# Layer 3's closing dot products as rows in column quarters of the array, two phases exchanged, and a new written order for layers 2 and 3 of a graph network

## The chip, the cores and the metric

The kernel runs on one core of a Trainium2 chip. The metric is the device time of one launch, in microseconds (us). The time before is 651.76 us, the median of three runs (651.25 to 652.19). The core has five engines that work side by side, each with its own instruction queue in program order: PE (TensorE, matrix products; its weight loads are listed as PEld), DVE (VectorE), ACT (ScalarE), POOL (GpSimd) and SP (SyncE, which here issues the DMA transfers).

## The reference, cut to what matters

Four graph layers run over the same 3327 nodes with 64 features and the same weighted adjacency matrix; each adds its result to x. Layer 0 is a gated graph convolution (two rounds), layer 1 a hyperbolic one, layer 2 one in which each row's neighbours are weighted by their rank from the end. The change is in layers 2 and 3. Layer 3, cut down:

```python
def _L3_gnn_ref(x, adj, att_W, att_b):
    x_tan = _logmap0(x, C)
    left = x_tan @ att_W[:D] + att_b
    right = x_tan @ att_W[D:]
    adj_att = jax.nn.sigmoid(left + right.T) * adj
    x_local = _logmap(x[:, None, :], x[None, :, :], C)
    support_t = jnp.einsum('ij,ijd->id', adj_att, x_local)
    return _proj(_expmap(x, support_t, C), C)
# layer 2
rank = jnp.cumsum(mask, axis=1)
w = mask * jnp.where(pos > 0, DECAY ** (k - pos), 0.0)
out = w @ (input @ weight) + bias
```

The logarithm map of a pair (i, j) depends on three inner products: of i with itself, of j with itself and of i with j. So the sum over j becomes a sum S_i of scaled neighbour vectors plus a single number d_i. What ends the layer is worked out per node from d_i and two dot products over the 64 features: h_i·S_i and S_i·S_i.

## The kernel before

**Nodes and groups.** The nodes are padded to 26 blocks of 128. Two blocks at a time are one column block c (0 to 12): the 128 partitions of a transposed tile hold the 64 features of both. Group 0 (`gs_`, the small group) is c = 0 to 5, group 1 (`gf`, the large one) c = 6 to 12.

**Layer 2.** For each of 52 steps n (26 source blocks for each group) there are: `mask` (L1784, DVE: which entries of an adjacency tile are set), `count` (L1815, PE: ranks by triangular products, into one of two PSUM pairs; then ACT or DVE turns ranks into powers of two, L1827 or L1825) and `weigh` (L1837, PE: these weights times the support rows, in two parts). The support itself is made by a chain of small steps, `support` (L1013 to L1063), a Python generator that a helper named `Weave` advances between the steps of a loop; the loop's `flush` holds a `weigh` back until its support is done. Up to step 27 this loop sets the order.

**Layer 3.** The symmetric pairs of column blocks are split into 13 `PHASES`; each phase names its direct columns (target ts from source c) and, derived from them, the turned ones (target c from source ts). For each phase m, half b and chunk there are `distances` (L1354, PE), `gelus` and `square` (ACT, or DVE), `tanh_d` and `tanh_t` (L1395, L1424, ACT), `attention_d` and `attention_t` (L1435, DVE, with the adjacency tile), `factors_d` (L1453, DVE), `turned` (L1469, PE transposes), `factors_t` (L1476, DVE), `gather_d`, `gather_t` and `singles` (all recorded at L1479, PE). The gathers add to S in four PSUM banks: `x0` and `x1` for the large group, `x2_` for blocks 0 to 3 and part of `ps_` for blocks 4 and 5. `singles` add the numbers d to 32-row quarters of `ps_`, four products beside each other in four quarters of the array's columns; those of the last phase's second half go to a bank of their own, `late_`, cleared by L1284.

**The order.** From step 28 of layer 2 on, the order of all these calls is a list written out by hand, `ORDER3`. An entry such as `gather_t.12.0.1` calls that step; `n`, `s`, `b`, `f` advance generators: `nodes3` of the two groups (normalisation, transposes, tables of layer 3; the small group's use POOL, L1145 to L1243), a bound, and `finish_f`. Each engine executes its part of the list in this order, so an instruction that waits holds up all behind it on its engine. The adjacency tiles are loaded by SP in the order in which `mask` and `attention` use them (`uses_of_tiles`), and a slot is filled again once its user is done.

**The end.** `finish_f` copies the large group's S to SBUF, multiplies it by the transposed h (`w1`) and squares it (`w2`), forms the dots with `added` (L1587: each block of w1 or w2 as 128-column weights, a moving operand `halves` of two columns that pick the upper and lower 64 features), and transposes S to node order (`by_nodes`, L1598). These steps stand in the list as `f`. After the list, `finish` does the same for the small group, copies the late single sums (`copied_singles`, L1604), brings them to node order (`picked`, L1609), and runs a chain of some 35 small DVE operations (L1656 to L1693) that ends in two scale factors per node; with these, ACT scales h (L1703), PE adds x (L1701, L1705) and DVE forms the output (L1708 to L1719), which SP stores.

Of the kernel before, what the change touches and what calls it, by code (L numbers as in the profile page):

```python
# [45 lines left out]

SLOTS3, SLOTS2, SLOTS1, SLOTS01 = 4, 7, 16, 19
# [126 lines left out]
for _c in range(0, 6, 2):  # L174
# [4 lines left out]
    Phase((0, r_(0, 4)), (1, r_(1, 4))),  # L179
    Phase((0, r_(4, 6)), (1, r_(4, 6)), (4, r_(4, 6)), (5, r_(5, 6))),  # L180
    Phase((2, r_(2, 6)), (3, r_(3, 6))),
# [21 lines left out]
def uses_of_tiles():  # L203

    last_first = [2 * c + h for c in reversed(range(HB)) for h in range(2)]
    layer2 = [(g, k) for g in (1, 0) for k in last_first]
    rest = []
    for name, *args in ORDER3:
        if name == "mask":
            rest.append(layer2[args[0]])  # L210
        elif name.startswith("attention"):
            rest.append((*args, name == "attention_t"))
    listed = sum(len(key) == 2 for key in rest)
    starts, uses = [], []
    for u in (
        FIRST + SECOND + THIRD + LAYER1,
        layer2[:NB],
        layer2[NB : len(layer2) - listed] + rest,
    ):
        starts.append(len(uses))  # L220
        uses += u
    return uses, starts[1:]
# [5 lines left out]
def order3(text):  # L228
# [14 lines left out]
    count.28.0 mask.30 count.28.1 mask.31 n n weigh.26.0 weigh.26.1 count.29.0 count.29.1 n  # L243
    n weigh.27.0 n weigh.27.1 count.30.0 count.30.1 weigh.28.0 weigh.28.1 weigh.29.0
    count.31.0 count.31.1 weigh.30.0 mask.32 mask.33 n weigh.29.1 count.32.0 mask.34
    count.32.1 weigh.30.1 weigh.31.0 count.33.0 count.33.1 mask.35 weigh.31.1 count.34.0
    count.34.1 weigh.32.0 weigh.32.1 weigh.33.0 weigh.34.0 n count.35.0 count.35.1 mask.36
    weigh.33.1 weigh.34.1 mask.37 count.36.0 weigh.35.0 count.36.1 count.37.0 n n n n n n
    weigh.36.0 weigh.35.1 mask.38 mask.39 count.37.1 mask.40 n n n count.38.0 count.38.1
    weigh.36.1 n weigh.37.0 count.39.0 weigh.37.1 mask.41 count.39.1 weigh.38.0 mask.42  # L250
    count.40.0 count.40.1 n weigh.38.1 count.41.0 weigh.39.0 weigh.39.1 weigh.40.0
    count.41.1 weigh.40.1 mask.43 count.42.0 count.42.1 n n n n weigh.41.0 weigh.41.1 n
    mask.44 mask.45 mask.46 count.43.0 count.43.1 n n n count.44.0 count.44.1 mask.47
    weigh.42.0 weigh.43.0 n n weigh.42.1 count.45.0 n n n mask.48 count.45.1 n weigh.43.1
    weigh.44.0 count.46.0 count.46.1 mask.49 weigh.44.1 count.47.0 n n n tanh_t.0.0.0
    count.47.1.1 weigh.45.0 n weigh.45.1 count.48.0 count.48.1 mask.50 weigh.46.0 mask.51
    weigh.46.1 count.49.0 weigh.47.0 tanh_t.0.0.1 tanh_t.0.1.0 count.49.1.1 weigh.47.1
    count.50.0 weigh.48.0 count.50.1.1 tanh_d.0.0 weigh.49.0 tanh_t.0.1.1 weigh.48.1
    count.51.0 count.51.1.1 weigh.49.1 distances.0.0.0 attention_t.0.0 gelus.0.0.0
    distances.0.0.1 weigh.50.0 weigh.51.0 gelus.0.0.1 attention_d.0.0 square.0.0 weigh.50.1  # L260
    weigh.51.1 wk evict distances.0.1.0 s s s tanh_t.1.0.0 gelus.0.1.0 tanh_d.0.1
    distances.1.0.0 gelus.1.0.0 distances.0.1.1 s clear.2 distances.1.0.1 gelus.0.1.1 s
    clear.1 factors_d.0.0 clear.0 square.0.1 gelus.1.0.1 gather_d.0.0 s s turned.0.0.0
    factors_t.0.0.0 distances.1.1.0 gather_t.0.0.0 turned.0.0.1 attention_t.0.1
    factors_t.0.0.1 gather_t.0.0.1 singles.0.0 s s tanh_d.1.0 turned.0.1.0 gelus.1.1.0
    factors_t.0.1.0 distances.1.1.1 s turned.0.1.1 attention_d.0.1 factors_d.0.1 square.1.0
    factors_t.0.1.1 gelus.1.1.1 distances.2.0.0 s s tanh_t.1.1.0 gather_t.0.1.0 s
    attention_t.1.0 attention_d.1.0 s s gelus.2.0.0 distances.2.0.1 s s square.1.1
    gather_t.0.1.1 turned.1.0.0 factors_t.1.0.0 tanh_d.1.1 attention_t.1.1 s s gather_d.0.1
    gelus.2.0.1 distances.2.1.0 factors_d.1.0 tanh_d.2.0 singles.0.1 gather_t.1.0.0  # L270
    gelus.2.1.0 turned.1.1.0 factors_t.1.1.0 square.2.0 distances.2.1.1 tanh_t.2.0.0
    gelus.2.1.1 s tanh_t.2.0.1 s gather_d.1.0 square.2.1 distances.3.0.0 s gelus.3.0.0
    gather_t.1.1.0 attention_d.1.1 factors_d.1.1 tanh_t.2.1.0 turned.2.0.0 distances.3.0.1
    gelus.3.0.1 tanh_t.2.1.1 singles.1.0 distances.3.1.0 square.3.0 attention_t.2.0
    factors_t.2.0.0 turned.2.0.1 gather_t.2.0.0 gelus.3.1.0 distances.3.1.1 attention_d.2.0
    factors_d.2.0 s s factors_t.2.0.1 turned.2.1.0 tanh_d.2.1 gelus.3.1.1 s gather_d.2.0
    tanh_t.3.0.0 tanh_t.3.0.1 distances.4.0.0 s s singles.2.0 singles.1.1 attention_t.2.1
    attention_d.2.1 factors_d.2.1 gelus.4.0.0 square.3.1 s s s factors_t.2.1.0 turned.2.1.1
    factors_t.2.1.1 distances.4.0.1 attention_t.3.0 turned.3.0.0 factors_t.3.0.0 tanh_d.3.0
    attention_d.3.0 s gather_d.1.1 s s turned.3.0.1 factors_t.3.0.1 gelus.4.0.1 s  # L280
    distances.4.1.0 s gather_t.2.1.0 tanh_t.3.1.0 gather_t.2.0.1 gather_t.3.0.0 tanh_t.3.1.1
    turned.3.1.0 factors_d.3.0 gelus.4.1.0 tanh_d.3.1 attention_t.3.1 attention_d.3.1
    tanh_d.4.0 s distances.4.1.1 gelus.4.1.1 factors_t.3.1.0 tanh_t.4.0.0 gather_d.2.1
    tanh_t.4.0.1 gather_d.3.0 gather_t.3.0.1 factors_d.3.1 singles.2.1 b turned.3.1.1
    attention_t.4.0 factors_t.3.1.1 distances.5.0.0 b gather_d.3.1 square.4.1
    attention_d.4.0 gelus.5.0.0 gather_t.3.1.0 square.4.0 tanh_t.4.1.0 gather_t.2.1.1
    distances.5.0.1 gelus.5.0.1 turned.4.0.0 tanh_t.4.1.1 z factors_t.4.0.0 distances.5.1.0
    factors_d.4.0 turned.4.0.1 singles.3.1 factors_t.4.0.1 tanh_d.4.1 gelus.5.1.0 square.5.0
    attention_t.4.1 singles.3.0 tanh_t.5.0.0 tanh_t.5.0.1 turned.4.1.0 attention_d.4.1
    factors_t.4.1.0 factors_d.4.1 distances.5.1.1 gather_t.4.0.1 gather_t.4.0.0 gather_d.4.0  # L290
    gather_t.3.1.1 turned.4.1.1 factors_t.4.1.1 gelus.5.1.1 attention_t.5.0 distances.6.0.0
    singles.4.0 tanh_d.5.0 attention_d.5.0 square.5.1 turned.5.0.0 gelus.6.0.0
    distances.6.0.1 tanh_t.5.1.0 tanh_t.5.1.1 gelus.6.0.1 factors_t.5.0.0 attention_t.5.1
    gather_t.4.1.1 tanh_d.5.1 gather_d.4.1 turned.5.0.1 distances.6.1.0 gather_t.4.1.0
    tanh_t.6.0.0 factors_t.5.0.1 gather_t.5.0.1 factors_d.5.0 gelus.6.1.0 turned.5.1.0
    square.6.0 distances.6.1.1 gelus.6.1.1 factors_t.5.1.0 singles.4.1 turned.5.1.1
    distances.7.0.0 attention_d.5.1 gather_t.5.0.0 tanh_t.6.0.1 factors_t.5.1.1
    gather_t.5.1.1 attention_t.6.0 square.6.1 turned.6.0.0 factors_t.6.0.0 gelus.7.0.0
    distances.7.0.1 gather_t.5.1.0 tanh_t.6.1.0 turned.6.0.1 gelus.7.0.1 tanh_d.6.0
    distances.7.1.0 factors_d.5.1 gelus.7.1.0 tanh_t.6.1.1 factors_t.6.0.1 attention_d.6.0  # L300
    singles.5.0 tanh_t.7.0.0 turned.6.1.0 attention_t.6.1 factors_t.6.1.0 tanh_d.6.1
    attention_d.6.1 distances.7.1.1 gather_d.5.0 gather_t.6.0.0 gather_t.6.0.1 gelus.7.1.1
    gather_t.6.1.0 gather_d.5.1 turned.6.1.1 tanh_t.7.0.1 distances.8.0.0 square.7.1
    square.7.0 factors_d.6.0 singles.6.0 factors_t.6.1.1 gelus.8.0.0 factors_d.6.1
    tanh_d.7.0 singles.5.1 attention_t.7.0 tanh_t.7.1.0 attention_d.7.0 singles.6.1
    turned.7.0.0 tanh_d.7.1 distances.8.0.1 gelus.8.0.1 gather_d.6.0 tanh_t.7.1.1
    factors_t.7.0.0 gather_t.7.0.0 tanh_t.8.0.0 tanh_t.8.1.0 factors_d.7.0 turned.7.0.1
    factors_t.7.0.1 attention_t.7.1 attention_d.7.1 distances.8.1.0 gelus.8.1.0
    gather_t.6.1.1 gather_d.7.0 turned.7.1.0 factors_t.7.1.0 tanh_t.8.0.1 distances.8.1.1
    singles.7.0 turned.7.1.1 tanh_d.8.0 gelus.8.1.1 distances.9.0.0 factors_d.7.1  # L310
# [107 lines left out]
def gnn_kernel(ctx: ExitStack, tc: tile.TileContext, t, out):  # L418
# [663 lines left out]

    ROWS = (HB + 1) // 2

    def by_halves(a):  # L1090
        return a.rearrange("p (c a) -> p a c", a=2)

    def gelu_table():

# [525 lines left out]
    def finish_f():  # L1620
# [9 lines left out]
        for lo in range(0, g.n, 2):  # L1630
            added(g, ws_, lo, min(lo + 2, g.n))
            yield
# [699 lines left out]
```

## Time and profile before

| | us |
|---|---|
| median of three runs | 651.76 |
| the profiled execution's own time | 650.47 |
| its span, first to last instruction | 648.7 |
| busy: PE / DVE / ACT / POOL | 605.6 / 450.8 / 378.5 / 24.4 |
| layer 2's first count (L1815) starts | 282.3 |
| layer 3's last factor product (L1453) ends | 623.61 |
| last gather ends | 625.68 |
| first operation of the closing DVE chain (L1656) starts | 631.46 |

Times are from the start of the span. "Busy" of PE is modelled: a product's record runs until its end, and products overlap. A product with 32-bit operands leaves two records. A table by stretches gives each engine's busy time within it, its instructions (x), the clock that PE was granted (1.00 is full), the share of the DMA engines' time and GB/s. The chain of waits follows the work that ended last back from the end: each piece is what the next one had to wait for. The mean granted clock over the span is 0.988.

### The profile page before, as it was taken

Reading aid. Unit: us, or ns where it says so; the run is one execution under the profiler, and the core shown is the slowest. Engines: PE = TensorE matmul, PEld = TensorE weight load, DVE = VectorE, ACT = ScalarE, POOL = GpSimd, SP = SyncE. Lnnn points to the kernel's source line nnn. Section 1 sums busy time; section 2 is a strip of 40 time slices with the busy share of each in tenths; the row PEclk is TensorE's granted clock in tenths of the full one; section 3 lists DMA queues with packets and bytes.
Section 4 is the critical chain, followed back from the end, with each engine's and each line's share of the span. In section 5 each row is a group of like instructions: output and inputs, shape, how many; then the busy total and the mean of one; then the engine's idle time right before and its main releaser. Section 6 shows DMA issues by size and latency. Waiting matters only on the chain.

```text
span 648.7 us, 13173 instructions
## 1 busy us (share of the span) xinstructions
PE 605.6 (93%) x5584; PEld 320.5 (49%) x5584; DVE 450.8 (69%) x688; ACT 378.5 (58%) x524; POOL 24.4 (4%) x44
## 2 busy tenths in 40 slices
PE   1988999999998999889999999999999999999992
PEld 1442334334333433346666776556556555555770
DVE  3240867444588750667655867899999999999855
ACT  3111300130254510458888979999999999999614
POOL 0000000000000000020000020027000000000000
PEclk9999999999999999999999999999999999999896
DMA  8999999459997899999878877437676766766301
GB/s 336 415 397 414 377 358 347 184 180 395 419 416 324 313 416 418 418 391 339 316 250 308 341 264 272 146 106 253 210 260 205 247 223 233 232 202 221 103 2 58
DMA packets 32531, 183.41 MB, mean 283 GB/s; under 512 B 3696, under 2 KB 4752, under 8 KB 32464
## 3 DMA queue, kind: packets, MB, share of 16 engines
q1 hardware_dynamic: 32112, 181.63, 74.9%
q0 software_dynamic: 352, 0.85, 0.5%
q8 instruction: 46, 0.75, 0.5%
q14 instruction: 21, 0.17, 0.1%
HBM read 180.76 MB, written 0.85 MB: 280 GB/s over the span
## 4 chain that ended last, share of the span: by engine, by line
PE 75%; DVE 9%; DMA 7%; ACT 5%; issue 2%; POOL 1%; SPq 0%; DVEq 0%; ACTq 0%
PE bank L757 25%; PE bank L1479 16%; PE pair L1815 8%; PE bank L1837 7%; PE pair L1354 6%; DMA adj<-in_adj 6%; PE pair L1469 4%; PE pair L858 2%; ACT w L1827 2%; PE bank L1587 1%; PE pair L662 1%; DMA xn<-in_x 1%; DVE edges L485 1%; DVE d L1435 1%; PE bank L1228 1%
## 5 line engine op out<-in xcount | busy, mean ns | idle before, releaser
L757 PE MATMUL bank<-adj,m_a 128*64 128x384 f32 (+1 forms) x832 | 154.6, 518 | 9.0 <-DMA adj<-in_adj 6.5
L757 PEld LDWEIGHTS bank<-adj,m_a 128*64 128x64 f32 x832 | 56.9, 137 | 96.5 <-issue 72.4
L1827 ACT ACTIVATE w<-pair,ebias 128x896 uint16<-128x896 f32 (+1 forms) x100 | 91.3, 953 | 14.6 <-PE pair L1815 13.8
L757 PE MATMUL bank<-adj,m_b 128*64 128x384 f32 (+1 forms) x416 | 76.7, 515 | 1.3 <-ACT hm L846 1.3
L485 DVE SCALAR_TENSOR_TENSOR edges<-adj,edges 128x1792 bf16<-128x1792 f32 (+1 forms) x24 | 45.0, 1890 | 32.0 <-DMA adj<-in_adj 31.9
L1784 DVE TENSOR_SCALAR mask<-adj 128x1792 bf16<-128x1792 f32 (+1 forms) x52 | 52.1, 1028 | 15.6 <-PE pair L1815 15.4
L846 ACT ACTIVATE hm<-bank 64x384 f32<-64x384 f32 (+1 forms) x8 | 4.1, 513 | 94.3 <-DVE mh L845 94.1
L1837 PE MATMUL bank<-w,m_b 128*64 128x384 bf16 (+1 forms) x416 | 56.0, 340 | 0.0
L757 PEld LDWEIGHTS bank<-adj,m_b 128*64 128x64 f32 x416 | 28.9, 137 | 45.5 <-issue 41.6
L1354 PE MATMUL pair<-xs 64*128 64x384 f32 (+3 forms) x120 | 50.2, 501 | 0.3 <-ACT s L1370 0.2
L1354 PE MATMUL pair<-xs,xw 64*128 64x384 f32 (+3 forms) x120 | 50.2, 501 | 0.1
L1395 ACT ACTIVATE d<-leftb,righth 128x768 f32<-128x768 f32 (+3 forms) x47 | 39.1, 893 | 0.2 <-PE bank L1479 0.2
L1435 DVE SCALAR_TENSOR_TENSOR d<-d,adj 128x1792 f32<-128x1792 f32 x19 | 38.4, 2019 | 0.3 <-ACT d L1395 0.3
L1837 PE MATMUL bank<-w,h_t 128*64 128x384 bf16 x208 | 38.0, 339 | 0.0
L1815 PE MATMUL pair<-mask,tri_b 128*64 128x384 bf16 (+1 forms) x208 | 37.4, 339 | 0.0
L1815 PE MATMUL pair<-mask,rest_a 128*64 128x384 bf16 x192 | 33.5, 341 | 1.7 <-ACT w L1827 1.6
L1479 PE MATMUL bank<-d,xd 128*64 128x384 f32 (+3 forms) x236 | 33.6, 426 | 0.0
L1837 PEld LDWEIGHTS <-m_b 128*64 128x64 bf16 x416 | 25.9, 110 | 12.2 <-issue 1.0
L1476 DVE SCALAR_TENSOR_TENSOR tr<-pair,tr 128x1024 f32<-128x1024 f32 (+3 forms) x28 | 26.7, 954 | 5.2 <-PE pair L1469 4.8
L1479 PE MATMUL bank<-d,p2c 128*32 128x128 f32 (+1 forms) x348 | 29.9, 322 | 0.0
L1424 ACT ACTIVATE tr<-leftb,righth 128x512 f32<-128x512 f32 (+1 forms) x48 | 29.3, 660 | 0.0
L1815 PE MATMUL pair<-mask,tri_a 128*64 128x384 bf16 x208 | 27.6, 341 | 1.4 <-ACT w L1827 1.3
(360 smaller groups left out, 1088.3 us busy)
## 6 DMA issues: line engine op xcount, KB each, us to landing
adj<-in_adj SPq DMA_DIRECT2D x108, 896.0 KB, 6.4
adj<-in_adj SPq DMA_DIRECT2D x94, 768.0 KB, 8.5
adj<-in_adj SPq DMA_DIRECT2D x8, 640.0 KB, 4.0
adj<-in_adj SPq DMA_DIRECT2D x2, 512.0 KB, 3.6
xn<-in_x SPq DMA_DIRECT2D x3, 192.0 KB, 5.0
out<-s SPq DMA_DIRECT2D x3, 192.0 KB, 2.4
xw<-xs POOLq DMA_DIRECT2D x4, 128.0 KB, 3.2
w_l<-in_w_l SPq DMA_DIRECT2D x1, 460.0 KB, 9.7
```

The lines of the kernel that those rows point to most:

```text
L485: V.scalar_tensor_tensor(e, a, 0.0, e, op0=OP.not_equal, op1=OP.add)
L757: T.matmul(acc[q][h * D : (h + 1) * D, : hi - lo], lhsT=m[:, k, :], rhs=a[:, h * g.w + lo : h * g.w + hi], start=first, stop=last,)
L1354: T.matmul(p[k][:, o : o + n], lhsT=l, rhs=r, start=not rows, stop=rows)
L1395: S.activation(columns(dirs[m, b], ph.n)[:, :, first * P : first * P + n], left_of(ph.g)[:, :, o : o + n], AF.Tanh, bias=righth[:, 2 * c + ...
L1424: S.activation(by_rows(a, m, u)[:, x : x + 2 * n].rearrange("p (b e) r c -> p b e r c", b=2), left_of(ph.s)[:, :, o : o + n * P].rearrange ...
L1435: V.scalar_tensor_tensor(a[:, :w], a[:, :w], 1.0, stream.tile(stream.now), op0=OP.add, op1=OP.mult)
L1476: V.scalar_tensor_tensor(a, p, rest_of(m), a, op0=OP.add, op1=OP.mult)
L1479: T.matmul(out, lhsT=lhsT, rhs=rhs, start=False, stop=True, skip_group_check=True)
L1784: V.tensor_scalar(masks[n][:, :w], a, 0.0, None, op0=OP.not_equal)
L1815: T.matmul(cnt[h][s * D : (s + 1) * D, P + lo : P + hi], lhsT=l, rhs=r, start=first and j == 0, stop=j == len(terms) - 1 or first and s == ...
L1827: S.activation(w, e, AF.Relu, bias=ebias)
L1837: T.matmul(acc2[i][q][h * D : (h + 1) * D, : hi - lo], lhsT=p[:, 2 * c + a, :], rhs=ws[n][:, h * g.w + lo : h * g.w + hi].bitcast(BF16), s ...
```

## The change

1. *Dots as rows.* `added` now takes a pair of column blocks r. It uses w1 or w2 as the moving operand (up to 256 columns) and a 32-column window of a zero-padded constant `hz` as weights, so that pair r's sums land in row r of a 32-row quarter. The four quarters hold (w1, w2) x (upper, lower half), as in `singles`. `hz` lies over a part of `w_all` that has no more readers then; POOL fills it at the start of layer 3. In `finish` the rows are copied to SBUF (`dd`, ACT) and two products with permuted columns of the identity bring them to node order.
2. *The last two phases are exchanged.* The last is now (0: 4-5), (1: 4-5), (4: 4-5), (5: 5); before it was (2: 2-5), (3: 3-5).
3. *A second generator, `finish_s`* (`e` in the list), copies, multiplies, squares and adds blocks 2 and 3, then 0 and 1, of the small group within the list; the product of blocks 2 and 3 is on POOL. Only blocks 4 and 5 are left to `finish`.
4. *The last single sums in two steps.* `singles.12.1.0` takes the turned columns, `singles.12.1.1`, after the last gathers, the direct ones; `picked(0)` moves from the first place to the second.
5. *The large group's `by_nodes`* moves from `finish_f` to `finish`, behind the products of the dots; its second part writes to the second bank of the pair that holds `late_`.
6. *The list* now begins at `count.0.0`, with `u` and `v` for the two `support` generators and a mark `l3` where layer 3's tiles are made; the loop, `flush` and the use of `Weave` in layer 2 go. Its whole order is new.

Cut to its core:

```diff
@@ PHASES
     Phase((0, r_(0, 4)), (1, r_(1, 4))),
+    Phase((2, r_(2, 6)), (3, r_(3, 6))),
     Phase((0, r_(4, 6)), (1, r_(4, 6)), (4, r_(4, 6)), (5, r_(5, 6))),
-    Phase((2, r_(2, 6)), (3, r_(3, 6))),
@@ ORDER3, first lines and last lines
-    count.28.0 mask.30 count.28.1 mask.31 n n weigh.26.0 weigh.26.1 count.29.0 count.29.1 n
...
-    attention_d.12.1 singles.11.1 singles.11.0 factors_t.12.1.0 turned.12.1.1
-    gather_t.12.1.0 gather_t.12.0.1 factors_t.12.1.1 gather_d.12.0 gather_t.12.1.1
-    factors_d.12.1 gather_d.12.1 singles.12.1 n s b f
+    count.0.0 count.0.1 u u u count.1.0 count.1.1 mask.2 mask.3 mask.4 u count.2.0 count.2.1
+    v count.3.0 count.3.1 u weigh.0.0 weigh.0.1 weigh.1.0 v mask.5 count.4.0 count.4.1
...
+    count.51.0 count.51.1.1 distances.0.0.0 distances.0.0.1
+    gelus.0.0.0 gelus.0.0.1 distances.0.1.0 attention_t.0.0 distances.0.1.1 weigh.49.0
+    weigh.49.1 gelus.0.1.0 gelus.0.1.1 weigh.50.0 weigh.51.0 attention_d.0.0 weigh.50.1
+    square.0.0 weigh.51.1 wk tanh_d.1.1 evict distances.1.0.0 gelus.1.0.0 attention_t.0.1
...
+    gather_t.12.1.1 singles.12.1.0 factors_d.12.1 singles.12.0 gather_d.12.1 gather_t.12.0.1
+    singles.12.1.1 e e e e n s b f f f f f e
@@ gnn_kernel
+    hz = w_all[:, : 2 * (31 + ROWS)].rearrange("p (h c) -> p h c", h=2)
@@ singles
-        if (m, b) == (n_all - 1, 1):
+        if step == 1:
+            picked(0)
+        if step == 0:
             ends_ = pair(0)
             sums_ = late_ = ends_[:, : 2 * P]
             cleared(late_)
             ds_ = ends_[:, 512:544]
-            picked(0)
@@ added
-    def added(g, ws_, lo, hi):
+    def added(g, ws_, r):
+        lo = (2 * r - g.c0) * P
+        n = min(2 * P, g.w - lo)
         for j, w in enumerate(ws_):
-            for i in range(lo, hi):
-                o = 32 * j + 2 * (g.c0 + i)
+            for h_ in range(2):
+                q = 32 * (2 * j + h_)
                 T.matmul(
-                    dots[:, o : o + 2],
-                    lhsT=w[:, i * P : (i + 1) * P],
-                    rhs=halves,
-                    start=True,
+                    drows[q : q + 32, :n],
+                    lhsT=hz[:, h_, ROWS - 1 - r : ROWS + 31 - r],
+                    rhs=w[:, lo : lo + n],
+                    start=(g, r) == (gf, gf.c0 // 2),
                     stop=True,
+                    skip_group_check=True,
                 )
@@ finish_s and finish
+        for E, c in ((G, 2), (V, 0)):
+            cs = slice(c * P, (c + 2) * P)
+            S.activation(m[:, cs], x2_[:, cs], AF.Copy)
             yield
+            E.tensor_mul(w1[:, cs], xs[:, cs], m[:, cs])
+            S.activation(w2[:, cs], m[:, cs], AF.Square)
+            yield
+            added(g, (w1, w2), c // 2)
+            yield
...
         copied_singles(1, late_)
-        for a, b, _ in parts_:
-            added(g, ws_, a // P, b // P)
+        added(g, (w1, w2), 2)
+        dd = flat(big(GROUPS[1], "sq"))[:, 4 * P : 6 * P]
+        S.activation(dd, drows, AF.Copy)
         picked(1)
+        v = dots.rearrange("p (j r i h) -> p i j r h", j=2, i=2, h=2)
+        for i in range(2):
+            T.matmul(
+                v[:, i],
+                lhsT=dd[:, i * P : (i + 1) * P],
+                rhs=ident.rearrange("p (j h k r) -> p j k r h", j=2, h=2, k=4)[:, :, 0],
+                start=True,
+                stop=True,
+            )
+        by_nodes(gf, late_f[0], bank(3), 0, 4)
+        by_nodes(gf, late_f[0], ends_[:, 5 * P :], 4, gf.n)
         by_nodes(g, m, pair(1), 0, g.n)
@@ layer 2
-        for n in range(len(work)):
-            mask(n + 2)
-            for part in range(2):
-                count(n, part)
-                flush(n, 2 if len(todo) > 2 * LAG + 2 else 1)
-                todo.append((n, part))
-                weave.tick()
...
+        take("l3")
```

## The prediction

> **What bounds the kernel.** I read the page first, then the table by stretches of time, then the chain of waits from 600 us, then the timelines of its end.
>
> The page, parts 1 and 2:
>
> ```profile
> PE 605.6 (93%) x5584; PEld 320.5 (49%) x5584; DVE 450.8 (69%) x688; ACT 378.5 (58%) x524; POOL 24.4 (4%) x44
> ...
> DVE  3240867444588750667655867899999999999855
> ACT  3111300130254510458888979999999999999614
> ...
> PEclk9999999999999999999999999999999999999896
> ```
>
> PE is busy nearly everywhere, but from slice 25 on (about 400 us, where layer 3 begins) DVE and ACT are at nine tenths as well. The clock row has an 8 near the end, which matters below. The stretches (columns: length, then busy time of PE, PE's weight loads, DVE, ACT, POOL, then granted clock):
>
> ```profile
> 281.00:409.00 128.00, 124.94 (x1409) 85.32 (x1411) 88.10 (x148) 109.56 (x135) 4.30 (x5) 1.00 0.83 304
> 409.00:428.00 19.00, 16.28 (x156) 8.37 (x160) 17.96 (x20) 18.21 (x29) 0.00 (x0) 1.00 0.28 81
> 600.00:623.61 23.61, 23.61 (x285) 16.55 (x283) 20.89 (x17) 11.10 (x15) 0.00 (x0) 0.93 0.22 72
> ```
>
> Layer 2 (281 to 409) is PE's: it has 3.1 us of visible idle time, DVE has 40. Layer 3 is shared: between 409 and 623.61 (the end of the last factor product) DVE is busy 205.65 of 214.61 us, so at most 9.0 us are to be had there by any ordering. At the end ACT has run out of work and PE carries it, as the chain of waits from 600 us says (start, length, what):
>
> ```profile
> 606.52 1.88 PE bank L1587 x16
> ...
> 613.74 1.43 PE bank L1587 x12
> 615.17 0.82 PE bank L1598 x7
> ...
> 625.68 0.23 PE pair L1284 x4
> 625.91 0.55 PE pair L1609 x4
> 626.45 1.64 PE pair L1479 x28
> 628.09 2.77 PE bank L1587 x24
> 630.86 0.47 PE pair L1609 x4
> 631.46 0.18 DVE d L1656
> ```
>
> The last gather into the accumulators ends at 625.68; the final DVE chain (L1656 on) starts at 631.46; from there to the end are 17.24 us that the change hardly touches. The 5.78 us between are all PE.
>
> **Part 1: dots as rows (L1587).** Before, 26 products with two columns each: 52 records of PE, at 1.88/16, 1.43/12 and 2.77/24 = 0.117 us each. That is 3.31 us for the large group (28 records, inside layer 3) and 2.77 us for the small one (after the last gather). A two-column product costs what its 128-column weight load costs. After, each pair of blocks is four products of 32 weight columns and 256 moving columns, in four column quarters. The nearest row is the single sums, which have just that shape: in the timeline four records (two "d", two "tr") go by every 0.22 us (626.40, 626.62, 626.84). Eight records are 0.43 us a pair. Large group: three pairs and a half one, 3 x 0.43 + 0.22 = 1.5 us, **-1.8**. Small group: 3 x 0.43 = 1.3 us, **-1.5**. What it adds behind: one copy of the sums to SBUF (128x256 on ACT, 0.38 us by L1604) and two products with full-width weights, 4 records x 0.117 = 0.47 us, with two hand-overs of some 0.1 us.
>
> **Part 2: what moves past the last gather.** The node transposes of the large group (L1598, seven, 0.82 us) go behind the products of the dots, where DVE's 4.8 us chain up to the first scaling (631.46 to 636.25) hides them with the next six and the identity products (L1701, 1.67 us): 1.5 + 1.7 = 3.2 of 4.8 us. If that cover failed they would cost at most their 0.8 us. **-0.8**.
>
> **Part 3: the last phases exchanged, single sums in two steps.** Sizes are the same (7 direct, 5 turned columns), only blocks 2 and 3 are complete a phase sooner and 0 and 1 before the last direct gather, so two thirds of the small group's copies, products and squares need not wait for it; ACT has the time (12.8 us idle before L1604), and one product goes to POOL. Of the late single sums (1.64 us), the turned part (640 of 1536 moving columns: 0.7 us) and the clearing (0.2) come ahead of the last factor product: +0.9 there. SP's loads of the two phases change places; DMA's share is 0.22 there. After the last gather PE then has: pick product 0.5, direct singles 0.9, three pairs of dots 1.3, the copy 0.38 with hand-overs 0.2, the two products 0.5 = **3.8 us, against 5.78: -2.0**. The ACT copy, square and DVE product of blocks 4 and 5 (0.38 + 0.38 + 0.42) lie beside the first 2.2 us of that.
>
> **Part 4: PE ahead of the last gather.** -1.8 (dots) - 0.8 (transposes) + 0.9 (turned singles, clearing) = -1.7. And the clock:
>
> ```profile
> 605.66:609.07 3.41, 3.41 (x46) 3.02 (x44) 3.11 (x3) 3.41 (x4) 0.00 (x0) 1.00 0.80 269
> 609.07:612.48 3.41, 3.41 (x22) 2.31 (x24) 3.16 (x2) 2.03 (x3) 0.00 (x0) 0.50 0.02 5
> ```
>
> For 3.41 us the clock is 0.50: sixteen gather records take 3.21 us there and 1.74 at 623.94. [...] The row says more: the 3.41 us before the drop hold the first 16 two-column products and the transposes around them, work that streams little. I take the row: with 256-column products in their place the drop goes, **-1.7**[...]. PE would be 3.4 us lighter ahead of the last gather. But DVE caps this: in 600 to 623.61 it idles 2.7 us, and from its last product to the last gather's end (2.07 us) some 1.2 remain necessary (half of the gather's products behind the second half of the factor, and one small turned gather). Cap 3.6; two nearly equal limits rarely give all: I take **-2.5** (ends -0.9 and -3.4).
>
> **The POOL product** (128x256) has no row of its size. Below: L1240-like small products, 0.20 us. [...]
>
> ```profile
> 440.92 1.16 POOL L1198 TENSOR_TENSOR par<-par,ab 128x48 f32<-128x48 f32 x1
> 442.14 1.90 POOL L1196 CAST ab<-par 128x48 bf16<-128x48 f32 x1
> ```
>
> Rows first: the same operations take 0.28 and 0.22 us at 440.27 and 440.62. POOL waits for DVE[...] while the DVE product beside the second (L1453 at 441.86) takes 2.10 instead of 2.02. By the row the change costs 0.1 us[...]. I take **+0.1**[...]. Its result is wanted only behind the direct singles, so POOL's own wait is covered by some 5 us.
>
> **Part 5: layers 2 and 3 listed anew.** The same instructions, other order. In layer 2 the first weighted product follows four counts instead of five and a half, because the last split of the support (L1062, L1063) no longer stands behind two masks on DVE (289.87 to 291.95 before); PE loses 1 to 2 us of counts as cover there and gets them back in products. Late in layer 2 all four distance chunks of the first phase stand ahead of the last weighted products instead of two, and a turned attention product ahead of the first factor: the stretch from 409 to 428, where PE idles 2.7 us, has more ready work. Masks, and so SP's tile loads, keep their sequence within layer 2; DMA's share is 0.83 there, no bound. POOL's transfers (L1161) keep their place behind the transposes. Bounds: nothing gained can exceed PE's 3.1 us in layer 2 plus DVE's 9.0 less the 2.7 already counted; a worse order could lose as much. I take **-1.5**, a quarter of DVE's remaining 6.3 us (ends -6 and +4).
>
> **Sum**: -2.0 - 2.5 + 0.1 - 1.5 = -5.9. The profiled execution took 650.47 us (span 648.7); it becomes 644.6. The median shown, 651.76, is 1.29 above it; the prediction on that scale is **646.0 us**, its own range 643.5 to 648.7.
>
> **Rivals.**
> (a) *The list yields most*: DVE's idle time in layer 3 is halved and layer 2 gains 2 us, -5 instead of -1.5: 642.3. For: both engines' gaps (L1476 waits 6.6 us for PE's transposes in 409 to 624) are matters of order. Against: a stretch at 97% of DVE leaves little.
> (b) *DVE's end governs*: its last product stays at 623.6, the PE savings ahead of it vanish and the list gives nothing: -2.0 - 0.9 + 0.3 = -2.6: 649.2. For: the single-sum and gather queue of PE at the end merely follows DVE. Against: DVE waits 1.5 us for a transpose at 613.8, so it follows PE.
> (c) *POOL's packing chain of the small group* (L1209 to L1218, 443.99 to 447.86), which feeds the transposes L1228 and with them phase 4. Between the eviction and phase 4's first distances the new list has 106 steps where the old had 119; if DVE's products lie denser there, each POOL operation can wait 1.9 us as above, and PE, which executes in order, stands behind L1228. Before, PE waited 0.3 us there. From 6 us of such waits on the change is a loss; six operations shut out, 11 us, less the 5.9: **656.9**. Against: several small ones fitted into one DVE gap before.
> (d) *Nothing to be seen*: losses of the list by 4 to 5 us cancel the end: 651.5.
> The change can't fail to do what it says: the dots must leave before the DVE chain.
>
> **Numbers.** Forecast 0.55, (a) 0.16, (b) 0.15, (c) 0.08, (d) 0.06. Range 640.8 to 650.8: it holds the forecast, (b) and most of (a). Within 0.2% (1.3 us) this kernel can't be told from unchanged: faster 0.86, same 0.06, slower 0.08.
>
> **What would show it.** Dots: pairs of blocks 0.43 us apart, not 0.9. End: last gather to DVE chain 3.8 us. Clock: no 0.50 stretch between 600 and 625. DVE: idle under 6 us from its first layer-3 product to the last factor. I am wrong if the first DVE operation of the final chain does not come about 6 us sooner, or if PE waits for POOL in layer 3.

## The result and the profile after

The changed kernel takes **646.03 us**, the median of ten runs (643.85 to 649.99), and the kernel before, run beside it on the same chip, 651.28 us (ten runs, 648.80 to 652.23). The ratio is 0.9932, with a 95% interval of 0.9913 to 0.9951. The forecast was 646.0 us. The profiled execution took 643.85 us (span 642.0) and is the fastest of the ten.

The total came out as forecast, but its parts did not. First the page of the changed kernel, parts 1 and 2 (busy time of each engine, then the granted clock in 40 slices):

```profile
PE 601.1 (94%) x5592; PEld 321.8 (50%) x5592; DVE 450.2 (70%) x687; ACT 378.4 (59%) x528; POOL 25.3 (4%) x48
...
PEclk9999999999999999999999999989999999999996
```

PE has 4.5 us less work, though it has eight records more. DVE and ACT have what they had. The 8 in the clock row has moved from the end to slice 27, where layer 2 passes into layer 3.

Then the stretches, cut at the same events as in the table below: first count, first layer-3 attention product on DVE, first factor product, 24 us before the end of the last factor product, that end. The columns are length, busy time of PE, weight loads, DVE, ACT and POOL, then the clock. First the changed kernel:

```profile
280.74:405.63 124.89, 123.76 (x1395) 89.27 (x1391) 88.03 (x148) 108.89 (x136) 5.18 (x8) 1.00 0.84 309
405.63:412.31 6.68, 6.68 (x64) 3.77 (x62) 6.68 (x6) 6.47 (x12) 0.00 (x0) 1.00 0.53 159
412.31:593.44 181.13, 178.58 (x2232) 103.07 (x2230) 175.27 (x136) 173.78 (x214) 15.08 (x29) 0.99 0.64 212
593.44:617.44 24.00, 23.89 (x348) 15.22 (x344) 23.37 (x19) 14.43 (x23) 0.95 (x1) 1.00 0.32 106
```

and the kernel before, cut at its own events:

```profile
282.32:409.38 127.06, 124.00 (x1405) 84.89 (x1403) 88.05 (x149) 109.94 (x136) 4.30 (x5) 1.00 0.82 302
409.38:418.49 9.11, 8.33 (x74) 4.32 (x70) 8.29 (x9) 8.54 (x13) 0.00 (x0) 1.00 0.53 161
418.49:599.61 181.12, 178.76 (x2260) 103.19 (x2258) 175.70 (x134) 174.03 (x218) 15.98 (x29) 1.00 0.64 213
599.61:623.61 24.00, 24.00 (x287) 16.65 (x284) 21.27 (x18) 11.49 (x16) 0.00 (x0) 0.93 0.24 77
```

Length less DVE's busy time is DVE's idle time. In the second stretch it falls from 0.82 us to nothing, and in the last 24 us from 2.73 to 0.63. In the long middle it is 5.42 before (181.12 - 175.70) and 5.86 after: the new list gave the middle of layer 3 nothing. The whole difference, stretch by stretch:

| stretch, us | before | after | difference |
|---|---|---|---|
| start to layer 2's first count | 282.32 | 280.74 | -1.58 |
| to the first layer-3 product on DVE | 127.06 | 124.89 | -2.17 |
| to the end of the last factor product | 214.23 | 211.81 | -2.42 |
| to the end of the last gather | 2.07 | 2.36 | +0.29 |
| to the closing DVE chain | 5.78 | 5.48 | -0.30 |
| to the end of the span | 17.21 | 16.70 | -0.51 |

The first row is the same work in both kernels; in two later executions of the changed kernel it was 283.19 and 284.33, so it is scatter. Over all fourteen traces of this case it lies between 280.74 and 285.28. The other rows make -5.11, close to the 5.25 between the medians.

What failed is the part behind the last factor product (617.44), where 2.9 us were forecast to go and none went. The chain of waits of the changed kernel there (start, length, what):

```profile
616.06 1.33 PE bank L1493 x24
617.39 0.02 issue
617.41 0.39 ACT sq L1625
617.80 0.04 issue
617.85 1.95 PE bank L1493 x20
619.80 0.55 PE pair L1630 x4
620.35 0.99 PE pair L1493 x14
621.34 1.29 PE bank L1607 x24
622.63 0.56 PE pair L1630 x4
...
623.28 0.39 ACT sq L1684
623.67 0.04 issue
623.71 0.63 PE bank L1688 x4
624.35 0.47 PE bank L1619 x4
624.82 0.34 PE pair L1619 x3
```

Up to 622.63 this is nearly the forecast, 2.83 us where 2.7 were reckoned: picking, direct single sums, three pairs of dots at 0.43 us each. Three things are not in it. The copy of the dots' rows (L1684) starts 0.65 us after the last dot. Between the identity products (L1688) and the chain stand 0.81 us of transposes by node (L1619), which the chain does not read. And ahead of the last gather PE stands 0.46 us for a copy of single sums (L1625). The view of single lines names what released the first two. For L1684 and L1706, the idle time of the engine and its releaser:

```profile
  PE pair L1630: 1.5, 1
```

```profile
  PE pair L1619: 4.6, 1
```

So the copy waits for the last picking products, and the chain's first product, which of what PE made reads only the single sums (`ds_`), waits for the transposes.

### The profile page after: what moved, and what is told of

The parts are those of the page before. It is cut to its first block, busy times and chain, and to the rows that moved or that the text cites. A ratio compares the mean times of both kernels' runs of the same rounds, so it can differ in the third digit from the quotient of the medians.

```text
span 642.0 us, 13208 instructions
## 1 busy us (share of the span) xinstructions
PE 601.1 (94%) x5592; PEld 321.8 (50%) x5592; DVE 450.2 (70%) x687; ACT 378.4 (59%) x528; POOL 25.3 (4%) x48
## 4 chain that ended last, share of the span: by engine, by line
PE 78%; DMA 8%; DVE 6%; ACT 5%; issue 1%; SPq 0%; DVEq 0%; ACTq 0%
PE bank L772 25%; PE bank L1493 18%; PE pair L1368 8%; DMA adj<-in_adj 8%; PE bank L1886 7%; PE pair L1864 7%; PE pair L1483 4%; PE pair L873 3%; ACT w L1876 2%; PE pair L677 1%; DMA xn<-in_x 1%; PE bank L647 1%; PE bank L1755 1%; ACT tr L1438 0%; DVE mask L1833 0%
## 5 line engine op out<-in xcount | busy, mean ns | idle before, releaser
L1886 PE MATMUL bank<-w,h_t 128*64 128x384 bf16 (+1 forms) x208 | 38.2, 339 | 0.1
L1493 PE MATMUL bank<-d,xd 128*64 128x384 f32 (+3 forms) x236 | 32.2, 411 | 0.5 <-ACT sq L1625 0.5
L1886 PEld LDWEIGHTS <-m_b 128*64 128x64 bf16 x416 | 27.3, 110 | 10.6 <-issue 1.5
L1493 PE MATMUL bank<-d,p2c 128*32 128x128 f32 (+1 forms) x348 | 28.5, 322 | 0.0
L1864 PE MATMUL pair<-mask,tri_a 128*64 128x384 bf16 x208 | 25.8, 341 | 0.7 <-ACT w L1876 0.7
```

Source lines behind the costliest of these rows:

```text
L1493: T.matmul(out, lhsT=lhsT, rhs=rhs, start=False, stop=True, skip_group_check=True)
L1864: T.matmul(cnt[h][s * D : (s + 1) * D, P + lo : P + hi], lhsT=l, rhs=r, start=first and j == 0, stop=j == len(terms) - 1 or first and s == ...
L1886: T.matmul(acc2[i][q][h * D : (h + 1) * D, : hi - lo], lhsT=p[:, 2 * c + a, :], rhs=ws[n][:, h * g.w + lo : h * g.w + hi].bitcast(BF16), s ...
```

## Experiments: the end

**The three waits.** In each edit the computation stays the same.

```diff
 # nodes_late: all three calls go behind the chain's product hu
-        by_nodes(gf, late_f[0], bank(3), 0, 4)
-        by_nodes(gf, late_f[0], ends_[:, 5 * P :], 4, gf.n)
-        by_nodes(g, m, pair(1), 0, g.n)
...
         V.tensor_sub(hu, e_, hu)
+        by_nodes(gf, late_f[0], bank(3), 0, 4)
+        by_nodes(gf, late_f[0], ends_[:, 5 * P :], 4, gf.n)
+        by_nodes(g, m, pair(1), 0, g.n)
```

> All 13 transposes by node of the closing are issued after the first nine products of the closing DVE chain instead of ahead of them. Theory A (the chain's start waits for transposes it does not read, because they write the PSUM tile that holds the single sums): from the end of the last gather to the chain's third product, the first that reads the dots, 5.75 us in the first profile, falls by the transposes' 0.81 plus the 0.27 of the two products that can then run ahead: 4.65 us; the whole time falls by about 1.1 us. Theory B (the chain waits for the products with the identity and their completion, the transposes only happen to end beside it): 5.75 us stays, time unchanged.

```diff
 # dd_same_tile: one buffer drawn once
-            pp_ = flat(big(GROUPS[1], "sq"))[:, : 4 * P].rearrange(...)
+            sq_ = flat(big(GROUPS[1], "sq"))
+            pp_ = sq_[:, : 4 * P].rearrange(...)
+            dd_ = sq_[:, 4 * P : 6 * P]
...
-        dd = flat(big(GROUPS[1], "sq"))[:, 4 * P : 6 * P]
+        dd = dd_
```

> The copy of the dots' rows writes the last third of the same drawn buffer as the copied single sums, instead of drawing that buffer a second time. Theory A (the second draw makes the copy wait for all readers of the first, so for the last picking products, which it does not need): the copy starts 0.1 us after the last dots' product (0.65 in the first profile), beside the picking products, and the closing chain starts 4.95 us after the last gather, not 5.48; time -0.5 us. Theory B (the copy waits for the PE to report the dots' products[...]): start 0.65 us after, 5.48 us stays.

```diff
 # all_three: both, and in the list
-    singles.12.1.0 factors_d.12.1 singles.12.0 gather_d.12.1
+    singles.12.0 singles.12.1.0 factors_d.12.1 gather_d.12.1
```

> Both edits together, and the single sums of the last phase's first half issued ahead of those of its second half's turned part, so that their copy, for which the last gather stands still 0.45 us, comes sooner. Theory A: from the last factor's end to the end of the last gather 2.36 us falls to 1.95, and from there to the closing chain's third product 5.75 falls to 4.1 (0.55 picking, 0.99 singles, 1.29 dots, 0.1, copy 0.39, 0.04, products 0.63, 0.1); the whole time is 2.0 us under the changed kernel's, ratio to the kernel before 0.990 or less. Theory B (these waits hide others of the same length, such as the transposes and the singles, which the PE has to run in any case before the end): at most 0.5 us of it reaches the end.

The changed kernel was timed beside them:

> The changed kernel as it is, timed beside its variants on the same chip. Expected: ratio to the kernel before 0.990 to 0.996, from the last layer-3 factor's end to the start of the closing chain 7.8 us as in the first profile (2.4 to the end of the last gather, 5.5 from there).

The chain of waits with the buffer drawn once, from the last gather's end:

```profile
620.38 0.55 PE pair L1632 x4
620.93 0.99 PE pair L1493 x14
621.92 1.29 PE bank L1609 x24
623.21 0.55 PE pair L1632 x4
623.76 0.60 PE bank L1690 x4
```

The copy has left the chain: it starts at 623.29, 0.08 us after the last dot, and runs beside the picking products; the identity products follow these at once. With all three edits:

```profile
620.43 1.88 PE bank L1493 x20
622.31 0.55 PE pair L1632 x4
622.86 0.99 PE pair L1493 x14
623.85 1.29 PE bank L1609 x24
625.14 0.55 PE pair L1632 x4
625.69 0.61 PE bank L1690 x4
```

Nothing is left but PE's own work. Measured:

| kernel | last factor to last gather | last gather to chain | to the chain's third product | ratio to before |
|---|---|---|---|---|
| changed | 2.36 | 5.48 | 5.67 | 0.9937 [0.9914, 0.9961] |
| nodes late | 2.36 | 3.51 | 4.68 | 0.9929 [0.9902, 0.9956] |
| one buffer | 2.36 | 4.91 | 5.11 | 0.9936 [0.9915, 0.9957] |
| all three | 2.14 | 3.51 | 4.12 | 0.9920 [0.9896, 0.9945] |

The third product is the first to read the dots. Theory A holds for both waits, within 0.05 us (4.65, 4.95 and 4.1 were expected). What stays open is whether the chain's wait goes by the whole tile or by a part of it: the single sums (columns 512 to 543) and the last three transposes (from column 640 on) lie in the same half of one tile of 1024 columns. Of the 0.4 us expected ahead of the last gather only 0.22 came: the copy's wait is gone, but PE now reaches the gathers only at 620.43, after the last factor product at 620.17. From the last factor product to the third product that is 6.26 us instead of 8.03. The whole time fell by less than the 2.0 us of theory A (medians 644.55 and 645.93). Both were run again on one chip:

> The version with all three edits once more, beside the changed kernel on the same chip: from the last factor's end to the chain's third product 6.3 us as in its first profile, ratio to the kernel before 0.990 to 0.993.

> The changed kernel on the same chip as the two versions above: from the last factor's end to the chain's third product 8.0 us, ratio to the kernel before 0.992 to 0.995, 1.5 us over the version with all three edits.

The intervals came back to the hundredth (6.26, 8.03), but the ratios were 0.9922 [0.9897, 0.9947] and 0.9915 [0.9893, 0.9936]: with six runs each, scatter of some 2 us hides 1.8. In the traces most of the gain does reach the end, against theory B: from the last factor product to the end of the span the two executions with all three edits take 23.01 and 22.82 us, three of the changed kernel 24.46 to 24.54. That the whole time beats the changed kernel's is not shown.

**The dots, both ways.** The old form put back into the changed kernel, and the new form alone put into the kernel before. The second is free of the two waits above: its copy writes to a buffer drawn once, and the three transposes that have to move go behind the chain's product `hu`.

```diff
 # old_dots, in added(); the copy and the identity products are left out
-                T.matmul(drows[q : q + 32, :n], lhsT=hz[...], rhs=w[:, lo : lo + n], ...)
+                T.matmul(dots[:, o : o + 2], lhsT=w[:, i * P : (i + 1) * P], rhs=halves, ...)
```

> The changed kernel with the dots of before alone put back: per pair of nodes two-column products into the bank of the dots, no copy of rows, no products with the identity. Its order is otherwise that of the changed kernel. Theory A (the dots as rows free the PE ahead of the last factors and with it the half-clock stretch): DVE's idle time in the last 24 us before the last factor, 0.63 us now and 2.73 in the kernel before, rises to 2.0 to 2.8; a stretch at half clock is back between 600 and 625 us; from the last gather to the closing chain's third product 5.67 becomes about 5.7 (dots 1.29 to 2.7, copy and identity products gone); in all +1.5 to +2.3 us over the changed kernel. Theory B (the new list places the dots where nothing waits, in either form): idle time 0.6 to 0.8, no half-clock stretch, +0.1 us in all.

```diff
 # rows_before, in added() of the kernel before; copy and identity products added, without the two waits
-                T.matmul(dots[:, o : o + 2], lhsT=w[:, i * P : (i + 1) * P], rhs=halves, ...)
+                    T.matmul(drows[q : q + 32, :n], lhsT=hz[...], rhs=w[:, i * P : i * P + n], ...)
...
-        by_nodes(g, m, b2, 4, g.n)
```

> The kernel before with the dots as rows alone (copy and identity products with them; the transposes of the large group's last three nodes go behind the chain's first nine products, since their bank now holds the rows; the copy writes the rest of the buffer of the single sums). Order, phases and single sums as before. Theory A: DVE's idle time in the last 24 us before the last factor falls from 2.73 to about 0.8, no half-clock stretch between 600 and 625 us, and from the last gather to the chain's third product 5.97 falls to about 5.0; 2.5 to 3 us under the kernel before, ratio 0.996. Theory B (the list, not the dots, freed the end): idle time stays over 2.2, only the 1.0 us behind the last gather goes, ratio 0.9985.

The last 24 us before the end of the last factor product, first with the old dots put back, then with the rows alone:

```profile
598.71:622.71 24.00, 23.97 (x318) 16.55 (x314) 22.87 (x19) 13.68 (x22) 0.74 (x1) 1.00 0.28 99
```

```profile
598.49:622.49 24.00, 22.90 (x309) 14.33 (x302) 23.14 (x20) 13.47 (x18) 0.00 (x0) 1.00 0.30 101
```

In the first the form costs 1.57 us more of PE ahead of the last factor products (28 records in 3.22 us, against 32 in 1.65). The rows alone did as theory A said: DVE's idle time (length less DVE's busy time) is 0.86 us, last gather to third product 5.00, ratio 0.9968 [0.9956, 0.9980]. With the old dots put back the idle time is 1.13 us, nearer to theory B, and the clock stays at 1.00. But the half-clock stretch comes later (windows of the same kernel, the last gather ending at 625.67):

```profile
626.89:630.30 3.41, 3.41 (x37) 3.16 (x29) 0.00 (x0) 0.38 (x1) 0.00 (x0) 1.00 0.02 5
630.30:633.71 3.41, 3.41 (x16) 3.13 (x16) 1.55 (x14) 0.00 (x0) 0.00 (x0) 0.50 0.00 0
```

The transposes by node ahead of the chain take twice as long there (0.94 + 0.65 us instead of 0.47 + 0.34). Last gather to third product is 6.68 us, where theory A had 5.7. In all 0.95 us to the last factor product (212.53 against 211.58, of the execution without a half-clock stretch there), 0.61 to the last gather and 1.01 behind it: 2.6 us. The ratio, 1.0010 [0.9993, 1.0027] against 0.9937, says some 4.7. Neither theory foresaw that; about 2 us of it are not located (the profiled execution took 285.28 us to the first count, but the work up to there is the same).

**POOL's product on DVE:**

```diff
-        for E, c in ((G, 2), (V, 0)):
+        for E, c in ((V, 2), (V, 0)):
```

> The changed kernel with the one 128x256 product of the closing that POOL makes given to DVE. Theory A (on POOL it costs DVE nothing, as the trace of the changed kernel reads): DVE takes 0.43 us more ahead of the last factors, of which its idle time there (0.63) can hold a part: last factor 0.2 to 0.4 us later. Theory B [...]: last factor 0.1 to 0.3 us sooner.

The last factor product ends 0.3 us later, counted from the first layer-3 product (212.12 against 211.81), as theory A said, and the last gather comes 0.33 sooner after it (2.03): together 214.15 against 214.17. Ratio 0.9936 [0.9914, 0.9958]. The product on POOL is neither cost nor gain here, and DVE is not seen to slow down beside it: in the changed kernel's trace the attention product that overlaps it (608.30 to 609.78) took the same 1.48 us as at 405.63. But it had begun before POOL's (609.43 to 610.38), and the other order did not occur.

## Experiments: the list

Two kernels exchange the heads of the lists, up to `evict`, and leave the rest.

```diff
 # layer2_old: the changed kernel's list
-    count.0.0 count.0.1 u u u count.1.0 count.1.1 mask.2 mask.3 mask.4 u count.2.0
+    mask.2 count.0.0 u count.0.1 u mask.3 count.1.0 u count.1.1 mask.4 count.2.0 u
...
     evict
```

> The changed kernel with layer 2 and the first steps of layer 3, up to the eviction of layer 2's last sums, in the order of the kernel before; every step after that as changed. Theory A (the new list wins its part ahead of the first layer-3 product on DVE, and layer 3, where DVE is the bound, carries it to the end): from layer 2's first count to that product 124.9 us becomes 127.1, DVE's idle time between it and the first factor 0.0 becomes 0.8, the rest stays: +2.5 to +3.0 us, ratio to the kernel before 0.997 to 0.999. Theory B (layer 3 waits later for something else, so that an earlier begin is given back as idle time): the first interval grows, DVE's idle time after the first factor, 5.9 us up to 24 us before the last, falls by as much; +0.5 us in all.

In the other, the kernel before takes these entries the other way round:

> The kernel before with only the head of the new list: layer 2 and the first steps of layer 3, up to the eviction of layer 2's last sums, in the order of the changed kernel; every later step, the dots, the phases and the end as before. Theory A (the head wins by itself): from layer 2's first count to the first layer-3 product on DVE 127.06 us becomes 124.9, and DVE's idle time from there to the first factor 0.82 becomes 0.0, the rest stays: 2.2 to 3.0 us under the kernel before, ratio 0.9955 to 0.9965. Theory B (head and rest are fitted to each other, as the 2.6 us of added idle time in the opposite exchange say): the head's 2.2 us are won, but DVE's idle time after the first factor rises from 5.4 by 2 us or more: ratio 0.998 to 1.001.

The first stretches of the changed kernel with the old head:

```profile
284.18:411.24 127.06, 124.00 (x1405) 84.91 (x1403) 88.01 (x149) 109.88 (x136) 5.65 (x8) 1.00 0.83 304
411.24:417.91 6.67, 6.36 (x54) 3.21 (x52) 6.67 (x6) 5.41 (x10) 0.00 (x0) 1.00 0.55 174
417.91:601.57 183.66, 178.77 (x2232) 103.14 (x2230) 175.30 (x136) 175.27 (x217) 14.93 (x29) 0.99 0.61 208
```

and of the kernel before with the new head:

```profile
284.19:409.10 124.91, 123.77 (x1395) 89.25 (x1391) 88.03 (x149) 108.90 (x136) 4.34 (x5) 1.00 0.84 308
409.10:420.48 11.38, 9.59 (x84) 5.42 (x80) 8.29 (x9) 10.41 (x18) 0.00 (x0) 0.91 0.41 129
420.48:600.99 180.51, 178.83 (x2250) 103.09 (x2248) 174.00 (x132) 170.19 (x212) 15.99 (x29) 0.99 0.64 211
600.99:624.99 24.00, 24.00 (x299) 16.46 (x301) 22.86 (x20) 13.17 (x17) 0.00 (x0) 1.00 0.30 100
```

The 2.15 us up to the first layer-3 product go with the head, in either kernel, to within 0.02 us: that part of theory A is shown. But the head is not worth 2.15 us by itself. The old head under the new rest does not show the 0.8 us of idle time that was expected ahead of the first factor product; it loses 2.5 us behind it as well (idle 8.36, not 5.86), so more than theory A said, and its ratio is 0.9995 [0.9979, 1.0010]. The new head under the old rest gains nothing: DVE's idle time is 3.09 us up to the first factor product and 6.51 after it, and the ratio is 1.0013 [0.9998, 1.0027]. Theory B describes this one. The waits of DVE name the seam, the place where head and rest meet (old head 411 to 432, new head 409 to 430; columns: us in total, times, longest):

```profile
DVE tr L1490 <- PE pair L1483: 2.8, 2, 2.4
```

```profile
DVE xn L1116 <- PE bank L655: 3.0, 2, 2.5
```

In the first DVE waits for the first turned transposes; in the second its steps for the nodes (`xn`) wait for products on PE. Both stand right behind the seam. In the second the 3.0 us are over at 418.16, before a half-clock stretch of 6.83 us begins at 418.49 (the 0.91 of the second line), so the clock did not make them. The last line of the new head's stretches shows one more thing. The closing steps there are those of the kernel before, in its order, yet the clock is 1.00 and DVE idles 1.14 us, not 2.73. So these steps do not bring the half-clock stretch of 609.07 with them every time. How often the kernel before has it at that place is not known: it was profiled once.

The exchange of the last two phases, the second generator and the single sums in two steps were not tried by themselves.

## An experiment on the clock

```diff
 # warm: all_three, and ahead of the closing's first identity products
+        for _ in range(3):
+            lo, hi, a = sums_x[0]
+            T.matmul(a, lhsT=ident, rhs=flat(xn[:, lo:hi]), start=True, stop=True)
```

> The version with all three edits, and three more 512-column identity products of PE (2.5 us at full clock, their result is overwritten) in the 3.85 us in which PE stands idle ahead of the closing's last products. Theory A (a stretch in which the array streams little is followed by one at half clock, whether by idle time or by narrow products): the clock stays at 1.0 through the closing, its last identity products take 1.7 us instead of 3.4; but DVE, busy with the outputs, waits for them only 0.37 us, so the whole time falls by 0.4 us at most. Theory B (the closing's half clock is on the path): 1.7 us come off. Theory C (the clock drops all the same): 3.4 us stay.

The closing's last identity products, with the filler and without it (least, median and longest of the four, in ns):

```profile
L1760 PE MATMUL bank<-s,ident x4: 486/591/697, 632.8 to 634.7; 128*128 128x512 f32 x2, 128*128 128x384 f32 x2
```

```profile
L1757 PE MATMUL bank<-s,ident x4: 847/895/1057, 631.5 to 633.7; 128*128 128x512 f32 x2, 128*128 128x384 f32 x2
```

And the stretch around them (632 to 635 us), again with the filler and without it:

```profile
632.00:635.00 3.00, 1.89 (x4) 0.59 (x4) 2.93 (x7) 3.00 (x14) 0.00 (x0) 1.00 0.20 71
```

```profile
632.00:635.00 3.00, 2.54 (x4) 0.50 (x2) 2.88 (x6) 2.27 (x10) 0.00 (x0) 0.50 0.23 76
```

With the filler PE's idle time ahead of these products is 1.28 us instead of 3.85, and in the one execution traced the clock stays at 1.00 (628 to 638 us). While the same products run in the traces of the kernel before, of the changed kernel and of the version without the filler, it is 0.50. So in this place the clock went with how PE was used just before. From the chain's third product to the last operation of DVE it is 10.64 us instead of 10.82, but to the end of the span 16.57 instead of 16.56: what follows DVE's last operation took 0.18 us longer, for a reason that is not known. So theory A: these 1.7 us are off the path; DVE is busy with the outputs meanwhile (2.88 of the 3.00 us). The ratio was 0.9898 [0.9876, 0.9920], which overlaps that of the version without the filler.

## Why the prediction was right in the sum and wrong in its parts

- **Part 1, the dots**: right. Pairs pass at 0.43 us (1.29 for three), and the three and a half of the large group take 1.65 us, where 1.5 were reckoned. (Before, eight 128-column weight loads take 0.97 us at 628.02, and their two-column products 1.05.) Alone, and without the two waits, they win 2.5 us between the medians (650.48 to 647.97).
- **Part 2, the transposes hidden behind the chain (-0.8), and Part 3, "3.8 us, against 5.78: -2.0"**: this is the step that failed. It came to 5.48 us. I summed PE's work and took the order as free of waits. But the last three transposes write the PSUM tile that also holds the single sums, so the chain waited for all seven (0.81 us), the case that the forecast had priced at "at most their 0.8 us" and did not count. And the copy drew its buffer a second time, so it waited for the readers of the first draw, the last picking products too (0.56 us). With both removed the chain starts after 3.51 us. Its third product, which like the 3.8 us includes copy and identity products, comes after 4.12: the work itself was sized to 0.3 us.
- **Part 4, "some 1.2 remain necessary"** from the last factor product to the last gather: 2.36 us. The copy that PE waits for was not in the sum, and twenty gather records (1.95 us) all come after the last factor product, not half of them. Ahead of that product DVE's idle time in the last 24 us fell by 2.10.
- **Part 4, the clock (-1.7)**: no such stretch came between 600 and 625 us, as said, but that the rows drove it away is only in part supported. With the two-column products in place it was also missing in two kernels (old dots put back, new head under the old rest), and DVE then idled 1.13 and 1.14 us in the last 24: of the 2.10 us some 1.6 go with the stretch and some 0.5 with the rest of the change. So it comes and goes, and I priced one execution. The mean clocks of single runs only hint at how often a stretch came. Of 46 runs of the kernel before on that chip 15 have 0.990 or more (median 649.76 us) and 31 less (651.14 us; 0.988 in the one profiled); of 17 with the rows alone 15 have 0.991 or more (0.991 in the one profiled, at 1.00 from 410 to 622 us). That speaks for the rows, but the means do not tell the stretches apart: that of the closing differs in length (12.4 us in the profile of the kernel before, 11.0 in that of the changed one), and an execution of the changed kernel with 6.82 us more at half clock has 0.990. In six traces with rows (three of the changed kernel, the rows alone, POOL's product on DVE, the old head) the clock is 1.00 over these 24 us; of the three with two-column products one has the stretch. In the kernel before (609.07) and with the old dots (630.30) half clock follows 3.41 us in which PE is recorded busy from end to end. That the drop would go with 256-column products was my estimate from one row.
- **Part 5, the list (-1.5)**: mis-sized. It won 2.17 us ahead of the first layer-3 product and 0.82 of DVE's idle time behind it, about 3, and nothing in the middle of layer 3. Head and rest win this only together. Rival (a) wanted 5 us of it.
- **POOL's product (+0.1)**: nothing measurable. Rival (c), POOL's packing chain, did not come: between 412 and 617 us PE waits, as far as can be seen, for DVE and ACT only, and most for this (columns as above):

```profile
PE pair L1483 <- DVE tr L1490: 1.8, 2, 1.3
```

Rival (b) came half true: behind DVE's last factor product nothing was won, but that product itself came 2.42 us sooner after the first layer-3 product.

That the sum was met is luck, a matter of errors that cancel. Behind the last factor product nothing came of 2.9 us; ahead of it the forecast held 3.0 us (-1.5, the other -1.6 of Part 4, +0.1) and 4.6 came; and the end of the span lies 0.5 us nearer to the chain's start, of which the forecast knew nothing. From the last operation of DVE to the end of the span it is 5.94 us before and 5.43 after; in eight traces this stretch, of which the last store is a part, varies from 5.4 to 6.0, and why is open. Besides, the forecast was to take 5.9 us off 651.76 (which makes 645.9); beside the changed kernel the kernel before ran at 651.28, and the gain is 5.25.

Of the prediction's own signs, the dots 0.43 us apart and the clock came true, and PE did not wait for POOL as far as can be seen. The 3.8 us did not come, nor did DVE's idle time under 6 us: it is 6.49 (0.00 + 5.86 + 0.63), against 8.97 before. The chain's first operation came 6.18 us sooner, as asked, but 1.58 of that is the scatter ahead of the first count; counted from there it is 4.60.

## What to carry to other kernels

Before work is counted as hidden behind a consumer, ask of each tile who else writes it: here a reader of one part waited for writers of another (0.81 us), and a second draw of a buffer waited for the last reader of the first (0.56 us), although the slices were apart. A written order should be tested as a whole: half of a good list under half of another lost everything either had won. And a stretch at half clock that is seen in one execution (here 3.41 us at 0.50) should be looked for in others before its removal is put into a sum.

## What was unexpected of the hardware

The changed kernel's half-clock stretch at the passage from layer 2 to layer 3 comes in some executions and not in others, of the very same program. (The two traces with the old list throughout, the kernel before and the rows alone, have none there: 1.00 from 410 to 598 us.) Two executions, 3.41 and 6.82 us long:

```profile
422.83:426.24 3.41, 3.41 (x30) 1.32 (x32) 3.41 (x3) 3.13 (x6) 0.00 (x0) 0.50 0.02 5
```

```profile
425.59:432.41 6.82, 6.82 (x66) 3.34 (x62) 6.19 (x11) 6.40 (x10) 0.98 (x3) 0.50 0.19 41
```

A third had none (1.00 from 408.10 to 619.68). DVE's idle time between the first factor product and 24 us before the end of the last is 5.67 us with none, 5.86 with 3.41 us at half clock and 7.11 with 6.82. The version with the old dots, in the same order there, had none and 5.68. The stretches fall differently from run to run; no run here shows the cause. Up to 1.4 us of idle time (7.11 against 5.67) go with them in one and the same program.
